# Where the taps of the convolution pause behind k, how LN2 spaces its last multiplications, when the sums of the next image are taken, and how the taps are shared out

## Chip, cores, metric

The kernel runs on one core of one Trainium2 chip. The metric is device time in microseconds of one execution; lower is better.

## What is computed

Eight images of 384 channels and 32 x 32 pixels pass through two layers. The first is an attention block over the 1024 pixels as tokens, the second a convolution block. Cut to what matters:

```python
# layer 0, tokens (1024 x 384), 8 heads of 48
xn = layernorm(x)                      # LN1
q, k, v = split(xn @ w_qkv.T + b_qkv)
out = softmax(q @ k.T * SCALE) @ v
x1 = x + out @ w_proj.T + b_proj
h = gelu(layernorm(x1) @ w_fc1.T + b_fc1)   # LN2, fc1: 384 -> 1536
x2 = x1 + h @ w_fc2.T + b_fc2               # fc2: 1536 -> 384
# layer 1
y = depthwise_conv_7x7(x2)             # 49 taps a channel
y = gelu(layernorm(y) @ w1 + b1)       # LN3, 384 -> 1536
y = grn(y) @ w2 + b2                   # global response norm, 1536 -> 384
out = x2 + y
```

All in fp32.

## The kernel before

**Tiling.** Channels lie on the 128 partitions in CT = 3 channel tiles, the 1024 tokens on the free axis in two halves of 512. A "product" below is TensorE work of U = 0.857 us in the plan: one full 128 x 128 matmul of 512 columns (the trace shows each as two records), or eight small matmuls of attention. Large linears use a scheme with 15 products in place of 18 blocks (`tiles_by_thirds`, `by_thirds`); q and k are made so, each in 15 products in the order `SINGLY` = 6, 10, 3, 5, 12, 2, 0, 11, 1, 4, 14, 7, 9, 8, 13. `behind(n)` is called with the number of the product, not with its place in that order: product 2 is the sixth, 0 the seventh, 7 the twelfth, 9 the thirteenth. The last two products of k are issued inside attention (`last_tile`). Results go out of the PSUM banks n, z, k, x by ScalarE copies (L470, L478) and VectorE adds (L473, L476); then a ScalarE bias (L648) finishes a whole tile of q or k.

**Order of the work.** [...]every engine runs its own list, and the lists are written by a planner, `Flow`. Each product adds its duration to `flow.now`; generators ("chains") hold the work of VectorE, ScalarE, POOL and DMA that goes on beside the products. A chain issues some instructions and yields how long it wants to wait; it is resumed behind the first product that ends past its due time. `flow.finish(chain)` issues the rest at once. So a number in a `yield` is not a wait on the chip, but a place in the lists.

**The stages of a middle image b (2 to 6).** The convolution of image b-1 runs beside the layer-1 linears of image b-2 and the first layer of image b: `grn_up` (w1), values of the image, `grn_down` (w2), q and k, attention (64 steps of scores, L804, Exp, L813, and product with v, L824), two `proj` (L746), LN2, fc1, fc2. VectorE and helpers share its 49 taps per channel tile:

- `convolution` issues VectorE taps (L1225, one tap of one channel tile of 1024 pixels each), paced by `us` and by `first`; it yields while the list `hold` is not empty.
- `help_convolution` takes the last `HELPED[ct]` taps of channel tile ct, tiles 2, 1, 0 in that order, in two halves each: ScalarE multiplies into one of four buffers (L1260) and POOL issues a DMA that accumulates it into `acc` (L1261). It pauses while the list `quiet` is not empty and three microseconds of plan beyond it; a tile is closed to `convolution` from the helper's first tap of it until 8 us after its last.
- `hold` is filled behind the twelfth product of k and emptied at the second scores of attention (`n == 1`); also in the two groups of the fast fc1 and over LN2 ("group", "ln2"). `quiet` is filled over `grn_down` and for two stretches of attention ("averages", from 23 and from 55 steps done), emptied behind each `proj`.

**LN2, the next image's LN1 and LN3.** `layernorm` makes a mean and a variance with matmuls against ones (L508; with folded halves L522), then three multiplications by scale and rstd (L582). In images 2 to 6 (`fast_fc1`) the second half of LN2 runs beside six plain fc1 tiles and the second `gelu_group` of 15 half-size products. Behind it stand, in this order: the adds of `norm_of_next` (LN1 of image b+1, L1967 and L1969), the end of the convolution (`end_convolution`: helper and taps finished at once), 11 us of plan, and LN3's adds (L541, L544), folds (POOL, L516), sums (L522), centring (L551), squares, variance. `norm_of_next(b, us)` takes its sums (L1961, four strips of 32 rows) `us` after its start, its variance later, and yields 45 us ahead of its final multiplications, which are needed by values of image b+1.

Of the kernel before, what the change touches and what calls it, by code (L numbers as in the profile page):

```python
# [64 lines left out]
CM = 2  # L65
NC = HT // CM
U = 0.857
HELPED = 6, 7, 7
BEGUN = 5
SCALE = HD ** -0.5  # L70
EPS0, EPS1, GRN_EPS = 1e-5, 1e-6, 1e-6
# [105 lines left out]
def block_kernel(  # L177
# [346 lines left out]
            totals.append((total, cols))  # L524
        return totals

    def layernorm(src, dst, h, eps, g, name, switch, spare=None, spaced=False, slow=1.0, fold=None, wait=3.4, gentle=False, late=0, lag=0, fold_squares=True):

        cols = h if isinstance(h, slice) else half(h)
        if isinstance(h, slice):
            h = h.start
        width = cols.stop - cols.start
        if spare:
            a, *squares = (t[:, :width] for t in spare())
            rstd = a
        else:
            a = one.tile([P, NH], F32, tag="ln_a", name=f"{name}_a{h}")[:, :width]  # L540
        nc.vector.tensor_tensor(a, src[:, 0, cols], src[:, 1, cols], ALU.add)  # L541
        if gentle:
            yield 1.2
        nc.vector.tensor_tensor(a, a, src[:, 2, cols], ALU.add)  # L544
        yield 2.6 * max(slow, 1.0)
        totals = yield from token_sums(a, f"{name}_sum{h}", fold, wait)
        yield 0.8
        for ct in range(CT):
            for total, part in totals:
                to, of = dst[:, ct, cols][:, part], src[:, ct, cols][:, part]  # L550
                nc.vector.scalar_tensor_tensor(to, total, -1.0 / C, of, ALU.mult, ALU.add)  # L551
            if gentle:
                yield 1.2
        yield 0.8 * slow + lag
        if not spare:
            squares = [three.tile([P, NH], F32, tag="ln_sq", name=f"{name}_sq{h}_{ct}")[:, :width] for ct in range(CT)]
        for ct in range(CT):
            nc.scalar.activation(squares[ct], dst[:, ct, cols], AF.Square)
            if spaced:
                yield 1.7  # L560
        yield 0.8 if spaced else 1.8 * slow
        nc.vector.tensor_tensor(squares[0], squares[0], squares[1], ALU.add)
        if gentle:
            yield 1.2
        nc.vector.tensor_tensor(squares[0], squares[0], squares[2], ALU.add)
        yield 1.8 * slow
        if not fold_squares:
            fold = None
            yield wait
        totals = yield from token_sums(squares[0], f"{name}_var{h}", fold, wait)  # L570
        yield 0.8

        if not spare:
            rstd = one.tile([P, NH], F32, tag="ln_rstd", name=f"{name}_rstd{h}")[:, :width]
        if switch:
            ln_table()
        for var, part in totals:
            nc.scalar.activation(rstd[:, part], var, AF.Ln, bias=eps, scale=1.0 / C)
        nc.scalar.activation(rstd, rstd, AF.Exp, scale=-0.5)
        yield (2.6 if switch else 1.2) * slow + late  # L580
        for ct in range(CT):
            nc.vector.scalar_tensor_tensor(dst[:, ct, cols], dst[:, ct, cols], col(g, ct), rstd, ALU.mult, ALU.mult)  # L582
            if gentle and ct < CT - 1:
                yield 1.2

    def averages():
        return [attn[:, i, :] for i in range(4)]
# [48 lines left out]
    def qk(b, xn, weights=None):  # L636

        big = large_tile(b)  # L640
        wqk_sb = wqk_in(big)
        parts = big[:, : 2 * NP * N].rearrange("p (i m n) -> p i m n", i=2, m=NP)
        moves = [(own, other) for i in range(2) for own, other in pieces(lambda m: parts[:, i, m, :])]

        def finish(i, m, src, cols=slice(0, N)):
            at = i * CT + m
            bias = bqk[:, at : at + 1]
            nc.scalar.activation(parts[:, i, m, cols], src, AF.Identity, bias=bias, scale=1.0 if i else SCALE)  # L648

        def move(i, m):  # L650
            for own, other in moves[2 * (i * CT + m) : 2 * (i * CT + m) + 2]:
                nc.sync.dma_start(out=own, in_=other)

        def args(i, m):
            return lambda k: wqk_sb[:, k, i * CT + m, :], lambda k: xn[:, k, :], CT

        def finishing(i, m):
            yield 1.7
            finish(i, m, parts[:, i, m, :])
            move(i, m)  # L660

        chains = {}

        def ready(m):

            for key in list(chains):
                if m in (key[1], NP - 1):
                    flow.finish(chains.pop(key))

        def plain(i, m):  # L670
            finish(i, m, linear(*args(i, m), f"qk_{b}_{i * CT + m}"))
            move(i, m)

        def fast(i):
            tiles = {}

            def bank(name):
                name = "x" if name in "jqm" else name
                if name not in tiles:
                    tiles[name] = o_tile(f"qk_{b}_{i}_{name}")  # L680
                return tiles[name]

            c = {f"c{r + 1}{n + 1}": parts[:, i, CT - 1 - r, half(n)] for r in range(CT) for n in range(2)}

            def behind(n):
                if i and n == 7:
                    hold.append("k")
                if n in (4, 9, 13):
                    m = (4, 9, 13).index(n)
                    chains[i, m] = flow.spawn(finishing(i, m))  # L690

            return tiles_by_thirds(weights, f"qk_{b}", i, thirds["qk"], c, bank, behind)

        def last_tile():

            if weights:
                flow.finish(rest_of_k)
                return
            for h in range(2):
                finish(1, CT - 1, linear_half(*args(1, CT - 1), h, f"qk_{b}_last_{h}"), half(h))  # L700
            move(1, CT - 1)

        if weights:
            for _ in fast(0):
                pass
            rest_of_k = fast(1)
            for n in rest_of_k:
                if n == 9:
                    break
            return parts[:, 0], parts[:, 1], last_tile, ready  # L710

        for m in range(CT):
            for i in range(2):
                if (m, i) != (CT - 1, 1):
                    plain(i, m)
        return parts[:, 0], parts[:, 1], last_tile, ready
# [76 lines left out]
    def attention(b, xt, qT, kT, last_tile, ready, first, next_image):  # L793
# [44 lines left out]
        for n in range(len(steps) + 2):  # L838
            if n == 1:
                hold.clear()  # L840
            if n == 2:
                last_tile()
            if n < len(steps):
                if steps[n][0] == 0 and steps[n][2] == 0:
                    ready(steps[n][1])
                ps[n] = scores(*steps[n])
            if n >= 2:
                product(*steps[n - 2], ps.pop(n - 2))
            if n - 2 in (len(steps) // 2 - 9, len(steps) - 9):
                quiet.append("averages")  # L850
            if n - 2 == len(steps) // 2 + 6:
                for chain in first:
                    flow.finish(chain)
                xn = one.tile([P, CT, N], F32, tag="xn", bufs=2, name=f"xn2_{b}")
                for m in (NP - 1, *range(CT)):
                    flow.finish(chains[0, m])
                proj(b, xt, 0)
                quiet.clear()
                next_image(b)
                slow = {1: 1.35, B - 1: 1.2}.get(b, 1.0)  # L860
                fold = "columns" if b else None
                ln = layernorm(xt, xn, 0, eps0, "g2", f"ln2_{b}", False, spaced=True, slow=slow, fold=fold, wait=4.5)
                if fast_fc1(b):
                    ln = sequence(ln, make_quarters(xn, hidden(b), 1.5))
                ln = flow.spawn(ln)
# [121 lines left out]
    def mlp(b, xt, xn, weights, tag, ln, rest, before_fc2=None, behind_ln=None):  # L987
# [9 lines left out]
        for m in range(HT // 2 if fast else HT):  # L997
# [5 lines left out]
            if m == (1 if fast else 3) and rest:  # L1003
                rest()
                slow = 0.8 if fast else 1.2 if b == 1 else 1.0
                if fast:
                    hold.append("ln2")
                ln = flow.spawn(layernorm(xt, xn, 1, eps0, "g2", f"ln2_{b}", True, slow=slow))
                behind_ln(ln)
        if fast:  # L1010
            gelu_group(hid, 1, b, weights, waiting)
# [817 lines left out]
    def main():  # L1829
# [60 lines left out]
        def conv_norm(b, ln):  # L1890
# [5 lines left out]
            else:  # L1896
# [1 line left out]
                how = dict(wait=5.0, late=3.5 if b > 1 else 0, fold_squares=b > 1) if b < B - 1 else dict(factor=2.4, slow=1.5, lag=4.0)  # L1898
                norm = abreast(acc, acc, eps1, "lnw", f"ln3_{b - 1}", True, **how)
                if b < B - 1:  # L1900
                    state["norm1"] = flow.spawn(after(ln, freely(norm_of_next(b, 22.0 if b > 1 else 28.0))))
                    state["norm3"] = flow.spawn(after(ln, freely(sequence(end_soon(b), norm))))
                else:
                    state["norm3"] = flow.spawn(after(ln, after(state["help"], after(state["conv"], norm))))
# [31 lines left out]
        def norm_of_next(b, us):  # L1936
# [62 lines left out]
            for h, a, _ in pairs:  # L1999
                for ps, view in sums[h]:  # L2000
                    nc.scalar.activation(view(a), ps, AF.Ln, bias=eps0, scale=1.0 / C)
                nc.scalar.activation(a, a, AF.Exp, scale=-0.5)
            yield 45.0
            for h, a, _ in pairs:
                for ct in range(CT):
                    part = xn[:, ct, half(h)]
# [257 lines left out]
```

## Time and profile before

| what | us |
|---|---|
| median of 3 runs | 3239.14 |
| lowest, highest | 3237.69, 3244.53 |
| profiled execution, its own time | 3245.64 |
| its span (first to last instruction) | 3243.9 |
| TensorE busy in it | 3213.5 (99%) |
| VectorE busy | 2540.3 (78%) |
| ScalarE busy | 1683.6 (52%) |
| POOL busy | 506.5 (16%) |
| all waits of TensorE for ScalarE at L648 / for VectorE at L473 | 8.6 / 8.0 |

The profile shows one execution. PE is TensorE, PEld its weight loads, DVE VectorE, ACT ScalarE, POOL GpSimd, SP the queue of most plain DMAs. A line of a timeline gives start, duration, engine, line of the kernel, operation, output <- input, shape, how many in a row, and in brackets the idle time ahead of it and what ended it. Matmuls overlap, so the time between two starts tells more than the durations. PEclk is the granted TensorE clock as a share of full speed.

### The profile page before, as it was taken

What the parts mean: (1) busy time and instruction counts of PE and PEld (TensorE: products, weight loads), DVE (VectorE), ACT (ScalarE), POOL (GpSimd) and SP (SyncE); (2) the same over time, 40 slices, a digit from 0 to 9 for tenths busy, and PEclk for the clock granted to TensorE, in tenths of its full rate; (3) what the DMA queues carried; (4) which work ended last, traced back from release to release, by engine and by line L of the source; (5) the groups of instructions that cost most, each with busy time, mean ns of one, the idle gap of its engine ahead of it and who ended that gap; (6) DMA issues with size and microseconds to landing.
All of it is one profiled execution on the core that took longest, in us unless ns stands there. A gap on an engine that the chain in (4) does not pass through costs nothing.

```text
span 3243.9 us, 39415 instructions
## 1 busy us (share of the span) xinstructions
PE 3213.5 (99%) x14204; PEld 1402.6 (43%) x14204; DVE 2540.3 (78%) x3578; ACT 1683.6 (52%) x2389; POOL 506.5 (16%) x607
## 2 busy tenths in 40 slices
PE   9999999999999999999999999999999999999999
PEld 5344434443444434444344443444435443344454
DVE  4548788897878978688777888778887788869964
ACT  3542763447644475453753637637375374742543
POOL 2102311012120121201212012120221202200000
PEclk9999999999999999999999999999999999999999
DMA  6525832557445564546636375363843638333244
GB/s 215 191 96 190 159 71 58 156 124 159 91 88 143 140 137 90 103 131 165 130 69 132 108 186 105 76 135 103 201 96 74 140 98 204 71 78 83 65 116 113
DMA packets 208741, 396.77 MB, mean 122 GB/s; under 512 B 42912, under 2 KB 49440, under 8 KB 208160
## 3 DMA queue, kind: packets, MB, share of 16 engines
q0 software_dynamic: 81984, 167.02, 27.2%
q1 hardware_dynamic: 126272, 226.49, 23.3%
q8 instruction: 114, 1.87, 0.2%
q10 hardware_dynamic: 288, 0.71, 0.1%
q14 instruction: 83, 0.68, 0.1%
HBM read 212.98 MB, written 40.11 MB: 78 GB/s over the span
## 4 chain that ended last, share of the span: by engine, by line
PE 86%; issue 5%; DMA 4%; DVE 3%; ACT 1%; POOL 1%; SPq 0%; POOLq 0%; DVEq 0%; ACTq 0%
PE fc L405 15%; PE s L804 13%; PE o L824 12%; PE fc_p L486 11%; PE o_p L486 6%; PE v L724 4%; PE proj L746 4%; PE h_n L457 3%; DMA acc<-tap 3%; PE h_z L457 3%; PE h_x L457 3%; PE h_last L1398 2%; PE o L1349 2%; PE h L392 2%; PE h_k L457 1%
## 5 line engine op out<-in xcount | busy, mean ns | idle before, releaser
L1225 DVE SCALAR_TENSOR_TENSOR acc<-pad,vec,acc 128x930 f32<-128x930 f32 (+8 forms) x808 | 905.5, 1157 | 5.7 <-DMA acc<-tap 2.5
L813 ACT ACTIVATE p<-s 128x1024 f32<-128x1024 f32 x512 | 523.9, 1025 | 250.3 <-PE s L804 242.3
L804 PE MATMUL s<-qk 48*64 48x512 f32 x4096 | 546.7, 592 | 10.0 <-ACT qk L648 8.6
L824 PE MATMUL o<-p,v 64*64 64x512 f32 x4096 | 541.8, 588 | 0.0
L405 PE MATMUL fc<-xn,fc 128*128 128x512 f32 x972 | 430.6, 599 | 0.0
L1261 POOL DMA_DIRECT2D acc<-tap x280 | 240.6, 873 | 1164.6 <-DVE gscale L1427 504.0
L486 PE MATMUL o_p<-y,w 128*128 128x512 f32 x664 | 289.0, 593 | 0.0
L804 PEld LDWEIGHTS s<-qk 48*64 48x64 f32 x4096 | 162.7, 133 | 289.1 <-issue 210.3
L405 PEld LDWEIGHTS fc<-xn,fc 128*128 128x128 f32 x972 | 185.5, 192 | 230.9 <-issue 224.6
L824 PEld LDWEIGHTS o<-p,v 64*64 64x64 f32 x4096 | 166.7, 132 | 274.3 <-issue 266.8
L486 PE MATMUL fc_p<-qk,fc 128*128 128x512 f32 x520 | 226.9, 593 | 0.0
L1260 ACT ACTIVATE tap<-pad,vec 128x512 f32<-128x512 f32 x280 | 206.3, 738 | 24.7 <-DMA acc<-tap 24.7
L486 PEld LDWEIGHTS o_p<-y,w 128*128 128x128 f32 x664 | 125.6, 190 | 157.7 <-issue 146.4
L1225 DVE SCALAR_TENSOR_TENSOR acc_last<-pad,vec,acc_last 128x377 f32<-128x377 f32 (+24 forms) x288 | 177.2, 688 | 0.6
L486 PEld LDWEIGHTS fc_p<-qk,fc 128*128 128x128 f32 x520 | 98.4, 190 | 123.6 <-issue 119.1
L498 ACT ACTIVATE qk<-fc,bfc_f 128x512 f32<-128x512 f32 x90 | 61.1, 684 | 141.9 <-PE fc L405 141.9
L498 ACT ACTIVATE hid<-fc,bfc_f 128x512 f32<-128x512 f32 x72 | 49.3, 687 | 159.1 <-PE fc L405 159.1
L765 DVE TENSOR_TENSOR attn<-o,attn 128x512 f32<-128x512 f32 x64 | 44.1, 689 | 110.9 <-ACT attn L763 109.2
L746 PE MATMUL proj<-attn,wproj_sb 128*128 128x512 f32 x288 | 127.3, 595 | 1.1 <-ACT b_f L1706 0.6
L974 ACT COPY pad<-x 128x512 f32<-128x512 f32 x42 | 26.4, 635 | 196.1 <-DVE x L1064 196.1
L724 PE MATMUL v<-wv_sb,xn 128*128 128x384 f32 x384 | 126.8, 487 | 0.0
L724 PEld LDWEIGHTS v<-wv_sb,xn 128*128 128x128 f32 x384 | 72.5, 190 | 50.1 <-issue 3.3
(445 smaller groups left out, 4610.3 us busy)
## 6 DMA issues: line engine op xcount, KB each, us to landing
acc<-tap POOLq DMA_DIRECT2D x280, 256.0 KB, 3.7
fc<-s_fc SPq DMA_DIRECT2D x91, 256.0 KB, 4.5
w<-s_w SPq DMA_DIRECT2D x91, 256.0 KB, 2.7
w<-s_w SPq DMA_DIRECT2D x72, 320.0 KB, 4.2
fc<-in_wfc SPq DMA_DIRECT2D x54, 384.0 KB, 4.2
y<-y POOLq DMA_DIRECT2D x38, 512.0 KB, 6.8
qk<-qk POOLq DMA_DIRECT2D x30, 512.0 KB, 7.4
qk<-s_qk SPq DMA_DIRECT2D x42, 320.0 KB, 5.1
```

Of the source, the lines that this page charges most:

```text
L405: nc.tensor.matmul(out=ps, lhsT=lhsT(k), rhs=rhs(k)[:, half(h)], start=(k == 0), stop=(k == nk - 1))
L457: nc.tensor.matmul(out=at, lhsT=weights.at(wname, g, slot // 5)[:, slot % 5, :], rhs=rhs[n], start=first, stop=True, skip_group_check=not ...
L486: nc.tensor.matmul(out=bank, lhsT=lhsT, rhs=rhs, start=k == 0, stop=k == len(pairs) - 1)
L498: nc.scalar.activation(dst, src, function, **kw)
L724: nc.tensor.matmul(out=ps[:, :C], lhsT=xn[:, k, t * P : (t + 1) * P], rhs=wv_sb[:, k, :], start=(k == 0), stop=(k == CT - 1),)
L746: nc.tensor.matmul(out=ps, lhsT=wproj_sb[:, m, ct * P : (ct + 1) * P], rhs=attn[:, m, :], start=(m == 0), stop=(m == CT - 1),)
L804: nc.tensor.matmul(out=s[64 * i : 64 * i + 64, j, :], lhsT=kT[64 * j : 64 * j + HD, m, k0 : k0 + 64], rhs=qT[64 * j : 64 * j + HD, m, half ...
L813: nc.scalar.activation(p, s, AF.Exp)
L824: nc.tensor.matmul(out=outs[i][64 * j : 64 * j + 64, :], lhsT=v[keys, t, at : at + 64], rhs=p[keys, j, :], start=(t == 0), stop=(t == KT - 1),
L1225: nc.vector.scalar_tensor_tensor(dst, window, tap, dst, ALU.mult, ALU.add)
L1260: nc.scalar.mul(t.rearrange("p (h w) -> p h w", w=W), window, tap)
L1261: nc.gpsimd.dma_start(out=acc[:, ct, half(h)], in_=t, accum_op=ALU.add)
```

## The change

Five edits. In the second half of `fast` (k), the helper is paused (`quiet`) behind product 2, the sixth, and the VectorE taps (`hold`) behind product 0, the seventh, instead of the VectorE taps alone behind product 7, the twelfth; both lists are emptied at the second scores. `HELPED` goes from 6, 7, 7 to 5, 7, 7, so that VectorE makes 44, 42 and 42 taps instead of 43, 42 and 42. LN2's three last multiplications of the second half are issued 1.3 us of plan apart in images 2 to 6 instead of in a row. The next image's sums are due 25 us instead of 22 us behind the start of its norm in images 2 to 6. Its final multiplications are due 42 us instead of 45 us behind the rstd, in images 1 to 6.

```diff
-HELPED = 6, 7, 7
+HELPED = 5, 7, 7
...
-    def layernorm(src, dst, h, eps, g, name, switch, spare=None, spaced=False, slow=1.0, fold=None, wait=3.4, gentle=False, late=0, lag=0, fold_squares=True):
+    def layernorm(src, dst, h, eps, g, name, switch, spare=None, spaced=False, slow=1.0, fold=None, wait=3.4, gentle=False, late=0, lag=0, fold_squares=True, apart=0):
...
             nc.vector.scalar_tensor_tensor(dst[:, ct, cols], dst[:, ct, cols], col(g, ct), rstd, ALU.mult, ALU.mult)
-            if gentle and ct < CT - 1:
-                yield 1.2
+            if (gentle or apart) and ct < CT - 1:
+                yield apart or 1.2
...
             def behind(n):
-                if i and n == 7:
+                if i and n == 2:
+                    quiet.append("k")
+                if i and n == 0:
                     hold.append("k")
...
             if n == 1:
                 hold.clear()
+                quiet.clear()
...
-                ln = flow.spawn(layernorm(xt, xn, 1, eps0, "g2", f"ln2_{b}", True, slow=slow))
+                ln = flow.spawn(layernorm(xt, xn, 1, eps0, "g2", f"ln2_{b}", True, slow=slow, apart=1.3 if fast else 0))
...
-                    state["norm1"] = flow.spawn(after(ln, freely(norm_of_next(b, 22.0 if b > 1 else 28.0))))
+                    state["norm1"] = flow.spawn(after(ln, freely(norm_of_next(b, 25.0 if b > 1 else 28.0))))
...
-            yield 45.0
+            yield 42.0
```

## The prediction

> **What bounds the kernel now.** I read the page first, for the engine that has no time left.
>
> ```profile
> PE 3213.5 (99%) x14204; PEld 1402.6 (43%) x14204; DVE 2540.3 (78%) x3578; ACT 1683.6 (52%) x2389; POOL 506.5 (16%) x607
> ```
>
> TensorE is busy for 3213.5 of 3243.9 us. The change removes no product, so it can win only TensorE's 30.4 us of idle time and whatever is hidden in "busy". The waits of TensorE, longest in total first, say where the idle time is:
>
> ```profile
> PE s L804 <- ACT qk L648: 8.6, 7, 2.4
> PE fc_n L457 <- DVE qk L473: 8.0, 5, 1.6
> PE ln_sum L1961 <- PE ln_sum L1961: 1.7, 5, 0.4
> ...
> PE s L804 <- ACT p L813: 1.4, 4, 0.5
> ```
>
> (total us, times, longest.) The first stands at the step from k to attention in the seven images 1 to 7, the next two in the images 2 to 6 that use the fast fc1. I then read the timeline at each place. Image 3, step to attention:
>
> ```profile
> 1143.62 0.74 ACT L1260 ACTIVATE tap<-pad,vec 128x512 f32<-128x512 f32 x1 [1.67 <-DMA acc<-tap]
> 1144.73 0.59 ACT L478 COPY qk<-qk_x 128x512 f32<-128x512 f32 x1
> 1145.35 0.69 DVE L473 TENSOR_TENSOR qk<-qk_n,qk 128x512 f32<-128x512 f32 x1 [2.49 <-ACT qk L478]
> 1147.85 0.74 ACT L1260 ACTIVATE tap<-pad,vec 128x512 f32<-128x512 f32 x1 [2.53 <-DMA acc<-tap]
> 1148.49 1.13 ACT L648 ACTIVATE qk<-qk,bqk 128x1024 f32<-128x1024 f32 x1
> 1149.68 1.95 PE L804 MATMUL s<-qk 48*64 48x512 f32 x16 [1.96 <-ACT qk L648]
> ```
>
> A helper's tap on ScalarE (L1260) waits for the landing of an older tap; the k copy and the bias (L648) that the first score needs stand behind it. The LN2 place, image 4:
>
> ```profile
> 1703.95 2.07 DVE L582 SCALAR_TENSOR_TENSOR xn<-xn,vec,ln_rstd 128x512 f32<-128x512 f32 x3
> 1705.93 0.41 DVE L473 TENSOR_TENSOR qk<-fc_n,qk 128x256 f32<-128x256 f32 x1
> 1706.40 0.70 PE L457 MATMUL fc_n<-xn,fc1t 128*128 128x256 f32 x2 [1.61 <-DVE qk L473]
> ```
>
> Three LN2 multiplications in a row delay the eviction (L473) that frees bank n. Last, the table of stretches (length, busy of PE, PEld, DVE, ACT, POOL, then PEclk) shows time that is called busy:
>
> ```profile
> 941.00:944.60 3.60, 3.60 (x6) 1.51 (x7) 3.60 (x7) 1.26 (x2) 0.00 (x0) 0.53 0.00 0
> 1738.00:1741.50 3.50, 3.50 (x10) 1.50 (x9) 3.50 (x8) 1.43 (x3) 0.00 (x0) 1.00 0.10 14
> 2736.60:2743.50 6.90, 6.66 (x20) 1.98 (x20) 2.31 (x3) 5.81 (x7) 2.54 (x3) 0.51 0.84 146
> ```
>
> After LN3's sums (L522) and the next image's sums (L1961), which stand back to back, the clock is about half for some 3.4 us in image 2 (first row), and likewise from 1340.5 (0.51) and 2528.4 (0.50), but not in image 4 (second row). The third row is the longest k wait, image 7: half the clock for 6.9 us.
>
> [...]
>
> **The change, part by part.** I followed the emission plan by hand (products of 0.857, taps and chains at their due times). For the old kernel it gives what the trace has: ten taps in the last burst, and the last helper tap just ahead of score 57 of the second pause.
>
> *Pauses behind k.* The ScalarE taps stop after the sixth product of k's second half, the VectorE taps after the seventh; until now ScalarE's never stopped and VectorE's stopped after the twelfth. Three helper taps (halves) and two VectorE taps move behind the first scores. The copy and the add of c31 then follow their products: product 10 ends 1144.7, add 0.69 with 0.17 ahead, L648 1.15: done by 1146.8, while TensorE is through its thirteenth product at 1147.2. The first score waits for nothing. From the end of the thirteenth product to the first score I read 0.1, 0.7, 2.1, 1.4, 1.5, 1.0 and 2.6 us (images 1 to 7), and 0.3 lost just before in image 3: **-9.7**. In image 7 the four products from the first score on took 7.0 us (2736.84 to 2743.85) against 3.8 in image 4, the halved clock: **-3.2**. The table load runs 1.5 us earlier, so the Exp waits (1.4, 2.2 with drains) shrink: **-1.3**. ScalarE's queue ahead of its next Exp is then as in image 1, where no Exp is late.
>
> *HELPED.* Per image two L1260 (0.738) and two POOL issues (0.873) go, one L1225 (1.157) comes; seven images: -10.3 on ScalarE, -12.2 on POOL, +8.1 on VectorE. None of the three ends a wait here by its sum. But the pause costs the helper about 10 us and the missing tap gives back 5 (two halves, 2.5 apart): by the plan 36 of 38 halves are issued before the pause at score 57, and two fall behind the second proj, during LN2, where ScalarE idles 2.3 us ahead of its squares. Price 0; without that idle time at most 0.74 for each.
>
> *The burst.* What VectorE has not done when LN2 ends is issued at once: ten taps now, twelve after (one counts as due just before). That is 2 x 1.157 = 2.3 us later for LN3's adds, their folds on POOL (L516), and TensorE's L522:
>
> ```profile
> 1713.66 11.57 DVE L1225 SCALAR_TENSOR_TENSOR acc<-pad,vec,acc 128x841 f32<-128x841 f32 x10
> 1728.81 1.33 POOL L516 DMA_DIRECT2D ln_a<-ln_a  x1
> 1729.36 1.62 POOL L516 DMA_DIRECT2D attn<-attn  x1
> 1734.62 1.07 PE L522 MATMUL ln_sum<-ln_a,ones 64*64 64x512 f32 x4
> ```
>
> The folds take 5.5 and 6.2 us to land because a 512 KB fc_e transfer (issued 1728.07, landed 5.3 later) is ahead of them; alone they take 3.4 to 3.6. The adds end 1726.7 and 1728.0; 2.3 later the folds go out near 1729.1 and 1730.4 and still end behind fc_e. Cover about 2 us: **+0.2** an image, +1; bounds 0 and 2.3 an image.
>
> *LN2 apart.* The adds of bank n then follow one multiplication (0.69): ready 1704.97 instead of 1706.35; the product waits 0.4 instead of 1.77 (1706.40 less its own 1704.63). The third multiplication ends near 1708.4, the first product that reads it comes after 1710: 5 x 1.3 = **-6.5**.
>
> *Next image's sums.* Due at 25 instead of 22, L1961 falls two full products behind L522. Its fourth product waits 0.35 for LN3's first centring (one bank serves both); that is then past: **-1.7**. [...]three half-clock windows at 3.4 x 0.5: **-5.1** in this execution. Everything of that norm moves with it: nine centrings (3.86), squares, two folds and four second folds of squares on POOL, ahead of fc2's own accumulates with about 3 us to spare. LN3's squares now precede them. Behind them wait bank s0 for fc2's first product and the gelu of fc1's tile 10: **+0.3** an image (+1.5), bounds 0 and 1.5. The multiplications stay at 67 for images 2 to 6 and come 3 us earlier in image 1, with no reader near: 0.
>
> Sum: -9.7 - 3.2 - 1.3 - 6.5 - 1.7 - 5.1 + 1 + 1.5 + 0.5 for the wider ScalarE/DMA reshuffle = **-24.5**. The profiled execution took 3245.64 (span 3243.9 and 1.7 around it), so 3221. It stands 6.5 above the median, 3239.14; its four clock drops, 8.3 us, can differ in each run, as three runs 6.8 apart suggest. Taken from the median with the fixed part (-19.2 + 3) and 3.4 for two drops: 3219.5. I take **3219.5**.
>
> **The rivals.** *Part comes back:* the two added taps show in full at L522 (2.3) and s0 is late (1.5) in five images: 19 instead of the 2.5 in my sum, 3219.5 + 16.5 = 3236, and 3228 where half of it shows. For it: VectorE runs without a gap from 1702 to 1728. Against: the fc_e transfer sets the landing now. *The pause doesn't empty ScalarE:* taps already queued still wait for landings, as the 0.95 ahead of the tap at 1140.72 shows; half of the k gain stays, 3219.5 + 7 = 3226.5. Against: that tap ends before the sixth product does. *Slower:* the two helper halves stay blocked until the burst. Its channel-tile-0 tap then waits for multiply, issue and landing, 0.74 + 0.87 + 3.7 = 5.3 us, and with the two added taps L522 comes 7.6 - 2 = 5.6 us late, in five images +28: 3239 - 19 + 28 = 3248. It decides where the second half has not landed when VectorE reaches that tap, the fifth of the burst, near 1719. By the plan it is issued 13 us of products before the burst, which speaks against. A *same* result needs some 3.3 us an image given back.
>
> **How the numbers follow.** Forecast 0.68, given back 0.12, half emptied 0.08, slower 0.07, near nothing 0.05. Runs of this kernel can tell a change of about 0.2%, 6.5 us. The first three lie beyond it mostly: faster 0.86, same 0.07, slower 0.07. The range 3211 to 3233 takes in all clock drops gone and no new cost (3239 - 19.2 - 8.3 = 3211.5), and rather more than half of the given-back case.
>
> **What the profile after would show.** Right: s <- qk L648 gone from TensorE's waits; fc_n <- qk L473 at 2 us or less in five; no half clock after the sums; TensorE busy near 3202 and a span near 3219; twelve or eleven taps in the burst; two taps on ScalarE in LN2. Wrong: TensorE waiting at L522 for a landing, fc2's first product waiting for xn's centring, or L648 still late.

## The result, and the profile after

The changed kernel takes **3221.03 us** (median of four runs, 3218.43 to 3224.02) beside 3241.84 for the kernel before in the same series: ratio as recorded 0.9931, 95% interval 0.9913 to 0.9949 (the two medians alone would give 0.9936). Forecast were 3219.5, with 3211 to 3233 as the range. The profiled execution took 3218.43, forecast 3221 for it, from 3245.64. The same kernel measured once more in a later series (e5 below) gave 0.9931 (0.9917 to 0.9946).

Line numbers move in the kernel after: scores L804 are L806, Exp L813 L815, taps L1225, L1260 and L1261 are L1228, L1263 and L1264, the next image's sums L1961 are L1964. L457, L473, L516, L522, L541, L582 and L648 stay.

First the page, busy time and share of each engine:

```profile
span 3216.7 us, 39370 instructions
PE 3201.6 (100%) x14204; PEld 1404.2 (44%) x14204; DVE 2547.9 (79%) x3585; ACT 1676.8 (52%) x2375; POOL 494.0 (15%) x593
```

The span is 27.2 us shorter. TensorE does the same 14204 matmuls in 11.9 us less busy time, and its idle time is halved, from 30.4 to 15.1. Most of the busy time is the clock: before, four stretches of 3.4, 3.4, 3.4 and 6.8 us ran at half clock and so lost 8.5 us; after, none did (the last 2 to 4 us of either kernel apart). TensorE's waits after, in total us, times and longest:

```profile
PE fc_n L457 <- DVE qk L473: 1.6, 6, 0.3
PE ln_var L522 <- DMA ln_sq<-ln_sq: 1.4, 2, 0.8
...
PE ln_sum L522 <- DMA attn<-attn: 0.6, 3, 0.2
PE ln_sum L522 <- DMA ln_a<-ln_a: 0.4, 1, 0.4
...
PE s L806 <- ACT qk L648: 0.2, 1, 0.2
```

The first score's wait fell from 8.6 to 0.2 (a wait in image 0, which was there before too), that of fc_n from 8.0 to 1.6; the wait inside the next image's sums and that for the Exp are gone. New are two waits at L522 for the folds, 1.0 in all. The timeline at the step to attention in image 3:

```profile
1140.48 0.69 DVE L473 TENSOR_TENSOR qk<-qk_n,qk 128x512 f32<-128x512 f32 x1 [1.95 <-PE qk_n L457]
1141.21 1.15 ACT L648 ACTIVATE qk<-qk,bqk 128x1024 f32<-128x1024 f32 x1 [1.07 <-DVE qk L473]
1142.38 1.28 ACT L494 ACT_TABLE_LOAD   x1
1142.88 1.95 PE L806 MATMUL s<-qk 48*64 48x512 f32 x16
1144.04 1.02 ACT L815 ACTIVATE p<-s 128x1024 f32<-128x1024 f32 x1 [0.38 <-PE s L806]
```

The bias L648 now waits for VectorE's add and for nothing else; it ends at 1142.36, the table load of 1.28 us follows it on ScalarE, and the first score starts at 1142.88 without a bracket, that is, without a wait. LN2 in image 4:

```profile
1689.78 0.74 DVE L582 SCALAR_TENSOR_TENSOR xn<-xn,vec,ln_rstd 128x512 f32<-128x512 f32 x1
1690.44 0.41 DVE L473 TENSOR_TENSOR qk<-fc_n,qk 128x256 f32<-128x256 f32 x1
1690.91 0.70 PE L457 MATMUL fc_n<-xn,fc1t 128*128 128x256 f32 x2 [0.28 <-DVE qk L473]
...
1691.98 0.74 DVE L582 SCALAR_TENSOR_TENSOR xn<-xn,vec,ln_rstd 128x512 f32<-128x512 f32 x1
```

One multiplication stands ahead of the eviction in place of three, and the product waits 0.28 instead of 1.61. Then the end of LN2, with the burst (the taps that VectorE has not done when LN2 ends, issued at once), LN3's adds, the fold and its reader:

```profile
1696.32 1.18 DVE L1228 SCALAR_TENSOR_TENSOR acc<-pad,vec,acc 128x930 f32<-128x930 f32 x1
...
1699.83 12.15 DVE L1228 SCALAR_TENSOR_TENSOR acc<-pad,vec,acc 128x870 f32<-128x870 f32 x11
1712.01 0.69 DVE L541 TENSOR_TENSOR ln_a<-acc 128x512 f32<-128x512 f32 x1
1712.58 1.19 POOL L973 DMA_DIRECT2D fc_e<-qk  x1 [3.94 <-ACT fc_e L972]
1714.62 0.85 POOL L516 DMA_DIRECT2D ln_a<-ln_a  x1 [0.86 <-DVE attn L541]
1719.57 1.08 PE L522 MATMUL ln_sum<-ln_a,ones 64*64 64x512 f32 x4 [0.38 <-DMA ln_a<-ln_a]
```

Eleven taps stand in the burst and a twelfth just ahead of it (first line), where the kernel before has ten and none: the twelve of the prediction, with the one that it counts as due just before. LN3's adds start 0.56 us ahead of the fc_e transfer's issue, before 2.81 ahead: 2.25 later, forecast 2.3. Last the table of stretches, with length, busy time of PE, PEld, DVE, ACT and POOL, then PEclk; two of image 2, from the next image's sums on, at the times at which the kernel before stood at half clock:

```profile
938.80:942.20 3.40, 3.27 (x15) 1.37 (x14) 3.24 (x6) 2.86 (x6) 0.00 (x0) 1.00 0.28 77
942.20:945.60 3.40, 3.40 (x9) 1.52 (x8) 3.19 (x8) 2.77 (x6) 1.43 (x2) 1.00 0.21 33
```

No half clock is left at the sums or behind k.

### The profile page after: what moved, and what is told of

It is laid out like the page before. It is cut to its first block, busy times and chain, and to the rows that moved or that the text cites. A ratio compares the mean times of both kernels' runs of the same rounds, so it can differ in the third digit from the quotient of the medians.

```text
span 3216.7 us, 39370 instructions
## 1 busy us (share of the span) xinstructions
PE 3201.6 (100%) x14204; PEld 1404.2 (44%) x14204; DVE 2547.9 (79%) x3585; ACT 1676.8 (52%) x2375; POOL 494.0 (15%) x593
## 4 chain that ended last, share of the span: by engine, by line
PE 92%; DMA 3%; issue 2%; DVE 1%; POOL 1%; ACT 1%; SPq 0%; POOLq 0%; DVEq 0%; ACTq 0%
PE fc L405 14%; PE s L806 12%; PE o L826 12%; PE fc_p L486 11%; PE o_p L486 11%; PE proj L748 4%; PE v L726 3%; PE h_n L457 3%; PE h_z L457 3%; PE h_x L457 2%; PE h_last L1401 2%; PE o L1352 2%; PE h L392 2%; PE qk_n L457 2%; PE qk_z L457 2%
## 5 line engine op out<-in xcount | busy, mean ns | idle before, releaser
L1228 DVE SCALAR_TENSOR_TENSOR acc<-pad,vec,acc 128x870 f32<-128x870 f32 (+8 forms) x815 | 911.1, 1157 | 2.7
L815 ACT ACTIVATE p<-s 128x1024 f32<-128x1024 f32 x512 | 524.3, 1025 | 256.7 <-PE s L806 248.1
L806 PE MATMUL s<-qk 48*64 48x512 f32 x4096 | 539.8, 590 | 0.2 <-ACT qk L648 0.2
L1264 POOL DMA_DIRECT2D acc<-tap x266 | 226.6, 857 | 1361.9 <-ACT tap L1263 678.8
L806 PEld LDWEIGHTS s<-qk 48*64 48x64 f32 x4096 | 163.9, 132 | 272.9 <-issue 206.0
L1263 ACT ACTIVATE tap<-pad,vec 128x512 f32<-128x512 f32 x266 | 195.1, 736 | 2.8 <-DMA acc<-tap 2.8
L1228 DVE SCALAR_TENSOR_TENSOR acc_last<-pad,vec,acc_last 128x377 f32<-128x377 f32 (+24 forms) x288 | 177.2, 690 | 0.6
```

The lines of the kernel that those rows point to most:

```text
L806: nc.tensor.matmul(out=s[64 * i : 64 * i + 64, j, :], lhsT=kT[64 * j : 64 * j + HD, m, k0 : k0 + 64], rhs=qT[64 * j : 64 * j + HD, m, half ...
L815: nc.scalar.activation(p, s, AF.Exp)
L1228: nc.vector.scalar_tensor_tensor(dst, window, tap, dst, ALU.mult, ALU.add)
L1263: nc.scalar.mul(t.rearrange("p (h w) -> p h w", w=W), window, tap)
L1264: nc.gpsimd.dma_start(out=acc[:, ct, half(h)], in_=t, accum_op=ALU.add)
```

## The experiments

Three series of four kernels; the kernel before ran beside each of them (medians 3246.0, 3245.1 and 3244.4), so ratios to it compare across series. One thing blurs medians of this kernel: near 140 us, in image 0, `proj` waits up to 3.2 us for VectorE's L793 (L791 in the kernel before), and a half-clock stretch of up to 6.8 us comes and goes behind it, whatever the kernel. So the table also gives, from each profile, the time from the first score of image 1 to the end of the span ("rest"), which leaves image 0 out. Medians of different series differ by a few us for the same kernel; the ratios allow for that.

| kernel | median us | ratio, 95% interval | rest |
|---|---|---|---|
| before (profile) | 3241.84 | | 2887.1 |
| after (profile) | 3221.03 | 0.9931, 0.9913 to 0.9949 | 2860.4 |
| e1: k's pauses undone | 3232.94 | 0.9960, 0.9947 to 0.9973 | 2875.1 |
| e2: LN2 not apart | 3225.05 | 0.9938, 0.9924 to 0.9953 | 2866.3 |
| e3: sums at 22 | 3222.97 | 0.9930, 0.9916 to 0.9945 | 2859.7 |
| e4: 6, 7, 7 helped | 3220.67 | 0.9922, 0.9907 to 0.9936 | 2858.6 |
| e5: after again | 3222.52 | 0.9931, 0.9917 to 0.9946 | 2860.9 |
| e6: ScalarE's pause only | 3222.55 | 0.9933, 0.9919 to 0.9947 | 2860.3 |
| e7: VectorE's pause only | 3236.05 | 0.9974, 0.9967 to 0.9982 | 2877.6 |
| e8: halves in the burst | 3227.89 | 0.9953, 0.9939 to 0.9966 | 2867.7 |
| e9: 3, 7, 7 helped | 3224.33 | 0.9938, 0.9925 to 0.9950 | 2863.7 |
| e10: before with sums at 25 | 3241.88 | 0.9992, 0.9984 to 1.0000 | 2886.4 |
| e11: before again | 3246.67 | 1.0006, 0.9998 to 1.0015 | 2883.7 |
| e12: ScalarE's pause, 6 helped | 3220.72 | 0.9929, 0.9916 to 0.9942 | 2861.8 |

### One part undone at a time

**e1**, the pauses behind k as before, all else changed:

```diff
-                if i and n == 2:
-                    quiet.append("k")
-                if i and n == 0:
+                if i and n == 7:
                     hold.append("k")
...
                 hold.clear()
-                quiet.clear()
```

> The changed kernel with the pauses behind k put back as they were (VectorE's taps alone pause, behind the twelfth product). Sum theory: the waits at the first scores come back, 9.7 us, with 1 us of late Exps, and in some executions 3.2 us of half clock in one image: 11 to 14 us slower than the changed kernel's 3221, so about 3233, and 9 faster than the kernel before. TensorE's wait s <- qk L648 is 7 to 10 us over seven images again. Rival (clock alone: all of the gain is half-clock windows gone, and removed waits only move): within 3 us of 3221. Plan: eleven taps in the last burst instead of twelve, no tap in LN2.

Measured 3232.94, the rest 14.7 longer than after; the first score waits 9.8 us for L648 (longest 3.6) and 1.3 for the Exp, and a half-clock stretch of 6.8 us stands at the first scores of image 3 (before: of image 7). The pauses behind k are about half of the gain: 14.7 of 26.7 us in the rest, 9.4 of 22 us by the ratios.

**e2**, LN2's multiplications in a row again:

```diff
-..., True, slow=slow, apart=1.3 if fast else 0))
+..., True, slow=slow, apart=0))
```

> The changed kernel with LN2's three multiplications in a row again. Sum theory: 5 x 1.3 = 6.5 us slower than the changed kernel, about 3227.5; the profile has fc_n <- qk L473 at 1.6 each, five times. Rival (a wait taken away there shows up later in fc1 or fc2, since VectorE is the engine behind): under 2 us slower.

Measured 3225.05, the rest 5.9 longer, and fc_n waits 8.2 us for L473 instead of 1.6. The two profiles say 6 us; the medians say 2.5 to 4, with intervals that hold both.

**e3**, the next image's sums at 22 again, the multiplications at 45 behind them:

```diff
-... norm_of_next(b, 25.0 if b > 1 else 28.0) ...
+... norm_of_next(b, 22.0 if b > 1 else 28.0) ...
...
-            yield 42.0
+            yield 45.0
```

> The changed kernel with the next image's sums at 22 and the final multiplications at 45 again. Sum theory: the 0.35 wait five times, 1.7 us, and half-clock windows after the sums in about three of five images, 5 us: 5 to 8 us slower, about 3228, with a wider spread between runs; the table of stretches shows PEclk near 0.5 at one to four of the five places. Rival (the windows come from chance, not from the place): 1 to 2 us slower and no half clock.

Measured 3222.97; the rest is 0.7 shorter. L1964 waits 0.5 us in all, and no half clock followed the sums in any image. In this place the edit bought nothing that shows in this run; why, is taken up with e10 and e11.

**e4**, six helped taps for channel tile 0 again:

```diff
-HELPED = 5, 7, 7
+HELPED = 6, 7, 7
```

> The changed kernel with six helped taps of channel tile 0. By the plan four helper halves instead of two fall into LN2, the last two ahead of ScalarE's rstd, and the last burst has eleven taps. Sum theory: 0 to 4 us slower (two taps of 0.74 in LN2's chain in five images, less one VectorE tap). Rival (this edit carries a good part of the gain by taking load from ScalarE and DMA): 5 us or more slower.

Measured 3220.67, the rest 1.8 shorter, and an interval that holds the 0.9931 of after: no gain of this edit shows either.

### Which of the two pauses it is

**e6** leaves VectorE's pause at the twelfth product, **e7** leaves ScalarE's out; **e5** is the changed kernel beside them.

```diff
# e6                                 # e7
-                if i and n == 0:    -                if i and n == 2:
+                if i and n == 7:    -                    quiet.append("k")
```

> The changed kernel itself, so that the next three stand beside it on one chip. 3221 (3218 to 3225); TensorE idle about 15 us, no wait of the first score for L648 above 0.3 us. If its gain came only from half-clock windows that happened to fall well, it would spread by several us and come near 3228 at times.

> Of the two pauses behind k only ScalarE's is moved (after the sixth product); VectorE's taps stop after the twelfth as before. My theory: the copy and the bias were late because they stood behind ScalarE taps that waited for landings, so this half holds nearly the whole gain: 3221 to 3224, eleven taps in the burst, s <- qk L648 at most 2 us. Rival, that both engines hold up the chain alike: the add of k (L473) falls behind a VectorE tap of 1.16 us in most images, L648 is late by about 1 us in seven, 3228.

> Of the two pauses only VectorE's is moved (after the seventh product); ScalarE's taps never stop behind k, as before. My theory: nothing gained over the kernel without both moves (3233), waits s <- qk L648 at 7 to 10 us, and twelve taps in the burst with cover for them: 3231 to 3235. Rival, both engines alike: half of the wait gone, 3227.

e6 is as fast as e5 (3222.55 and 3222.52), e7 13.5 slower. The timeline of e7 at image 3 shows the cause in the tap at 1144.95:

```profile
1140.41 0.58 ACT L478 COPY qk<-qk_x 128x512 f32<-128x512 f32 x1 [0.26 <-PE qk_x L457]
...
1144.95 0.74 ACT L1261 ACTIVATE tap<-pad,vec 128x512 f32<-128x512 f32 x1 [3.96 <-DMA acc<-tap]
1145.60 1.13 ACT L648 ACTIVATE qk<-qk,bqk 128x1024 f32<-128x1024 f32 x1
1146.79 3.33 PE L804 MATMUL s<-qk 48*64 48x512 f32 x16 [2.98 <-ACT qk L648]
```

ScalarE stands idle for 3.96 us, because a tap at the head of its queue waits for a buffer whose accumulate has not landed; the bias behind it has had its data since 1142.03, when VectorE's add ended. The scores that then start take 3.33 for what is 1.95 at full clock. In e6 a VectorE tap is back beside k's last adds, and costs nothing:

```profile
1142.22 1.18 DVE L1228 SCALAR_TENSOR_TENSOR acc<-pad,vec,acc 128x930 f32<-128x930 f32 x1
1142.34 1.15 ACT L648 ACTIVATE qk<-qk,bqk 128x1024 f32<-128x1024 f32 x1 [1.07 <-DVE qk L473]
1143.31 0.68 DVE L473 TENSOR_TENSOR qk<-qk_z,qk 128x512 f32<-128x512 f32 x1
1143.91 0.68 DVE L476 TENSOR_TENSOR qk<-qk,qk_k 128x512 f32<-128x512 f32 x1
1144.01 1.95 PE L806 MATMUL s<-qk 48*64 48x512 f32 x16
```

The tap follows the add that L648 needs and delays only later adds, and no first score waits (0.2 us for L648 in all, in image 0). The rival that both engines count alike (3228 for e6, 3227 for e7) falls.

### The burst, its cover, and the slower rival

**e8** makes the slower rival true: in images 2 to 6 the pause of ScalarE's taps ends only when the burst is issued, so the two late halves go out in it.

```diff
-            quiet.clear()
+            if not fast_fc1(b):
+                quiet.clear()
...
+                if fast_fc1(b):
+                    quiet.clear()
                 flow.finish(state["help"])
                 flow.finish(state["conv"])
```

> The changed kernel with the pause of ScalarE's taps not ended after score 57's stretch in the five images of the fast fc1, but only when the burst is issued: the helper's last halves go out in the burst, as in my slower rival. By that rival's own price the fold at L522 comes 5.6 us late in five images: 3221 + 28 = 3249, with TensorE waiting at L522 for a landing about 5 us in each. If VectorE does not stand at the tap of channel tile 0 (the half landed, or its order in the burst leaves time), the delay is that of the landing alone beyond the cover of 2 us: at most 1.7 in each, 3229. If the burst has more cover than I reckoned: 3221.

**e9** lengthens the burst with nothing else late: HELPED = 3, 7, 7.

> The changed kernel with 3, 7, 7 helped taps in place of 5, 7, 7: the burst at the end of LN2 grows from eleven to fourteen taps, VectorE reaches LN3's adds 3 x 1.157 = 3.5 us later. By the cover in my prediction (2 us, of which the eleventh tap has taken 1.2) L522 comes 2.7 us late in five images: 3221 + 13 = 3234. By the cover that the run with the blocked halves showed (3.6 us late, 1.3 of it at L522, so 2.3 left) it is 1.2 in each, 3227. If the length of the burst costs nothing at all: 3221.

e8 first, the burst in image 4 on VectorE, POOL and TensorE:

```profile
1705.42 4.23 DVE L1229 SCALAR_TENSOR_TENSOR acc<-pad,vec,acc 128x870 f32<-128x870 f32 x4
1712.89 8.03 DVE L1229 SCALAR_TENSOR_TENSOR acc<-pad,vec,acc 128x928 f32<-128x928 f32 x7 [3.24 <-DMA acc<-tap]
...
1723.55 0.85 POOL L516 DMA_DIRECT2D ln_a<-ln_a  x1 [4.18 <-issue]
...
1726.41 1.07 PE L522 MATMUL ln_sum<-ln_a,ones 64*64 64x512 f32 x4 [1.63 <-DMA ln_a<-ln_a]
```

VectorE stops at the fifth tap of the burst, the place that the rival named. But the stop is 3.24 us and not 5.3, although the landing takes 5.4 us where the price had 3.7: ScalarE multiplies from 1702.66 on, and the first four taps run while the halves travel. TensorE then waits 1.63. In all five images, from its waits:

```profile
PE ln_sum L522 <- DMA ln_a<-ln_a: 7.5, 5, 2.3
```

That is 7.5 us, where 28 were priced; the rest is 7.3 longer than after. In e9 the burst has thirteen taps, not fourteen: LN3's adds start 1.61 us behind fc_e's issue, 2.2 later than after and not 3.5. TensorE waits 2.0 us in five images; the rest is 3.3 longer, the median 3224.33. The prices of 13 and of 6 us were both too high. Why, is in the landing times of the fold (queue totals around the burst in image 4: KB each, us from issue to landing), of after, e9 and e8:

```profile
ln_a<-ln_a POOLq DMA_DIRECT2D x1, 128.0 KB, 4.8
```

```profile
ln_a<-ln_a POOLq DMA_DIRECT2D x1, 128.0 KB, 3.2
```

```profile
ln_a<-ln_a POOLq DMA_DIRECT2D x1, 128.0 KB, 2.7
```

The later the fold went out behind the 512 KB fc_e transfer in these three, the sooner it landed. fc_e is issued at 1712.58 after and at 1716.11 in e9, and lands 5.1 and 5.2 later; the fold is issued 2.0 and 3.6 behind fc_e, and lands 1.8 and 1.6 behind fc_e's landing, so 6.8 behind its issue in both. Only in e8, issued 5.4 behind it, does its own 2.7 count. TensorE is ready for L522 6.6 us behind fc_e's issue in all three. So the wait has three parts. A fold issued 0.74 behind fc_e (before) or 1.4 (four of the five images after) cost nothing; issued 2.0 behind it (image 4 after) it cost 0.38 us and 3.6 behind it (image 4 of e9) 0.3, and the longest of the five waits is 0.6 in e9; issued 5.4 behind it (image 4 of e8) it cost 1.63, and the longest wait of e8 is 2.3. From these numbers I estimate that every further microsecond counts from about 6.6 - 2.7 = 3.9 on. From the 0.74 of before, the cover is then about 3.2 us and not 2, at a price of about half a microsecond at most.

### What the sums' place is worth

**e10** is the kernel before with e3's edit the other way round (25 and 42), **e11** the kernel before again.

> The kernel before with one part of the change alone: the next image's sums at 25 in place of 22, the multiplications at 42 after them. By my sum: the wait of 1.7 us inside the sums gone and the half-clock windows behind them gone, 5.1 in a run that has three: 3.4 to 6.8 below the kernel before, 3239. Rival, that the windows fall on the place by chance (about one in three of five places) and that only the wait goes: 1 to 4 below, 3242. The waits at k and at LN2 stay at about 8.6 and 8.0 us.

> The kernel before once more, for its half-clock windows: in the first profile they followed the sums in three images of five. If the place of the sums makes them, they come again in the same three images (2, 3 and 6). [...]

e10 is 2.6 us faster than before by the ratio (0 to 5.2), in the range of the lower expectation, though the interval reaches into the other's; its wait inside the sums is gone, and those for L648 (9.2) and at fc_n (8.0) stand as before. e11 shows how the clock differs from run to run. In the first profile of before half-clock stretches followed the sums of images 2, 3 and 6; in this one it is image 6 alone. TensorE there, then the stretch behind the sums in image 6, and the end of the sums with what follows in image 3:

```profile
2528.59 1.08 PE L522 MATMUL ln_sum<-ln_a,ones 64*64 64x512 f32 x4
2529.71 1.08 PE L522 MATMUL ln_sum<-attn,ones 64*64 64x512 f32 x4
2530.72 0.71 PE L1961 MATMUL ln_sum<-ln,ones 32*128 32x256 f32 x6
2531.70 0.80 PE L1961 MATMUL ln_sum<-ln,ones 32*128 32x256 f32 x2 [0.27 <-PE ln_sum L1961]
2532.43 7.79 PE L405 MATMUL fc<-xn,fc 128*128 128x512 f32 x14
```

```profile
2532.00:2535.40 3.40, 3.40 (x6) 1.42 (x5) 3.40 (x7) 1.26 (x2) 0.00 (x0) 0.52 0.00 0
1343.00:1346.40 3.40, 3.02 (x15) 1.16 (x12) 3.40 (x7) 0.00 (x0) 0.00 (x0) 1.00 0.00 0
1346.40:1349.80 3.40, 3.40 (x10) 1.49 (x9) 3.40 (x9) 2.70 (x5) 0.00 (x0) 1.00 0.27 80
```

No full product runs from 2528.59 to 2532.43, 3.84 us; call this the dip. The next 3.4 us are at half clock. The dip is in the same place in all five images; whether a half-clock stretch follows differs from run to run. Of 15 such places in the three profiles with the sums at 22 (before, e3, e11) four had one; of 55 in the eleven with the sums at 25, one. That one is e8's image 3, where TensorE first waits:

```profile
1331.21 1.08 PE L522 MATMUL ln_sum<-ln_a,ones 64*64 64x512 f32 x4 [1.67 <-DMA ln_a<-ln_a]
1332.24 1.12 PE L522 MATMUL ln_sum<-attn,ones 64*64 64x512 f32 x4
1333.29 3.59 PE L405 MATMUL fc<-xn,fc 128*128 128x512 f32 x4
```

1.67 of idle time and 2.1 of small sums make a dip of 3.75 us (1329.54 to 1333.29), and PEclk is 0.52 from 1333.0 to 1336.4.

The profile of before has a record of each change of the granted clock. Its half-clock stretches start at 941.236, 1340.595, 2528.433 and 2736.646 us and last 3.413, 3.413, 3.413 and 6.827 us; the distances between their starts are 117, 348 and 61 times 3.4133. So in this profile they all lie on one grid with steps of 3.4133 us.

The five dips of this profile, in images 2 to 6, are 3.91, 3.71, 3.70, 3.69 and 3.85 us long. In images 2 and 6 a whole step of the grid lies within the dip (937.82 to 941.24 and 2525.02 to 2528.43), in image 3 all but the last 0.34 us of one, and the half clock starts where that step ends. In images 4 and 5 the step that comes nearest begins 1.5 and 0.7 us ahead of the dip, and the clock stays full. At 25 the dips are shorter: 2.2 to 2.6 us in the profile of after, where no half clock follows any. That is what the edit does for the clock, besides the wait of 1.7 us. That place and chance both have a part, the one by the length of the dip, the other by where the grid lies in a run, is my estimate from these five dips; for the other profiles it is not shown. In e3 the sums are back at 22, the dip of image 2 is 3.70 us long (936.57 to 940.27), and no half clock follows it or the other four.

### The smaller change

**e12** keeps of the change only what paid or was not tried apart: VectorE's pause at the twelfth product, 6, 7, 7 helped taps.

> The changed kernel less the two parts that bought nothing: VectorE's pause behind k back at the twelfth product, and 6, 7, 7 helped taps. From the two runs that undid them one at a time: 3220 to 3222, no difference from the changed kernel that can be measured. If the two parts needed each other (a VectorE tap ahead of k's add, and more helper halves late in LN2) it is slower, 3226.

Measured 3220.72, ratio 0.9929. No difference from the changed kernel can be measured: it is as fast with two edits fewer.

## Why the prediction was right, point by point

**Pauses behind k, -14.2: right in size and in mechanism.** By e1 it is 14.7 in the rest, 11.9 in the median and 9.4 by the ratio; by e7 against e5, which differ in ScalarE's pause alone, 16.7 in the rest and 13.5 in the median. Of its terms, the waits for L648 and Exp were 8.4 and 1.4 in the trace (9.7 and 1.3 in the sum). The prediction puts the seven waits of 8.6 us on images 1 to 7; they are those of images 2 to 7 and one of 0.2 in image 0, which stays. The term for the halved clock, 3.2, was read from one place in one execution; the five profiles without ScalarE's pause lose 3.4 to 6.8 there, in image 3, 7 or both, and the nine with it nothing. It was the right size for a single run, and the image that it falls on differs between the five. The sum did not divide the two pauses; e6 shows that VectorE's is worth nothing.

**HELPED, 0: right, as far as can be told.** e4 lies 0.4 below after in the median, 2.9 by the ratio and 1.8 in the rest; its interval holds the ratio of after, so neither a gain nor a loss is shown. Two ScalarE taps did fall into LN2, in its idle time.

**Burst, +0.2 an image: right, with its cover mis-sized.** L522 waits 1.0 us in all, 0.2 an image, and VectorE is 2.25 us later, as the sum had it. The reason was the right one too: the fc_e transfer ahead sets the landing (the fold lands 6.8 us behind fc_e's issue in after and in e9). But the cover is about 3.2 us, by my estimate, and not 2, since the first fold alone lands in 2.7 us (e8) and not in 3.4 to 3.6. The small waits stand within the cover (0.4 us in image 4, the rest at the second fold), and not at its end, where the sum had them; that both came to 0.2 an image is luck.

**LN2 apart, -6.5: right by the traces.** fc_n's wait fell by 6.4; e2 gives 5.9 in the rest, and 2.5 to 4 in medians whose intervals hold 6.5.

**Next image's sums, -6.8: the term that was mis-sized.** The wait of 1.7 is gone (e10's and the changed kernel's waits). The -5.1 for three half-clock stretches is what these two executions differ by, but as the worth of the edit it is too much: the sum took the stretches as made by the place alone, and e3 has the sums there and none, e11 one. The full products between the sums did shorten the dips, from 3.7 to 3.9 us before to 2.2 to 2.6 after, and no half clock followed them in after. By the count, 4 of 15, five images have 1.3 of them on average, at half of 3.4 us each 2.3 us, a rough estimate from three profiles; e10 has 2.6 for wait and clock together (0 to 5.2), where the sum had 6.8 from the execution and 5.1 from the median.

**Bank s0 and gelu behind the moved work, +1.5: not there.** TensorE's waits show none for fc2's first product.

**The sum.** The profiled execution became 27.2 us shorter, forecast were 24.5. The two costs that did not come, 2 us at s0 and in the reshuffle, are most of the difference in size. By kind it fits less well: busy time fell by 11.9 where the clock terms had 8.3, idle time by 15.3 where the waits had 19.2 less 3 of new ones; the 3.6 more of busy time I can't assign to a line. The median fell by 18.1 from the 3239.14 that the forecast started from, 19.6 forecast; that start was a low draw of three, and beside runs of the same series it is 20.8 to 22.6.

**The rivals.** *Part comes back:* no, L522 waits 1.0 in all. *The pause doesn't empty ScalarE:* no, the last tap ahead of the bias of image 3 waited 0.58 us for a landing, but started at 1136.02, five us ahead of the bias. *Slower:* its stop at the fifth tap is real (e8), but the halves were issued in time, and its price was nearly four times too high (28 for 7.5 us): it let multiply, issue and landing start only when VectorE was already waiting, and kept the cover at 2.

## What to carry over

ScalarE worked its list in order in these timelines: in e7 it stood idle for 3.96 us at a tap, with the bias behind it whose data had been there since 1142.03. A list that mixes critical copies with filler that may wait on a transfer should have no filler before the critical stretch; ask which of the engines holds filler that can *block*, because filler that only takes time (VectorE's taps here, 3222.55 in e6 beside 3222.52 in e5) did no harm. The fold that queued behind the larger fc_e transfer could be issued later at little cost (at most 0.6 us in e9, up to 2.3 in e8, where its own landing time counted), so measure cover from the transfer ahead. A half-clock stretch in one trace is one draw (4 of 15 like places here had one): compare the dip ahead of it with the dip that the change leaves (3.7 to 3.9 us and 2.2 to 2.6 here), and count over several profiles before the stretch is priced as removable.

## What was not expected of the hardware

TensorE's clock was halved behind dips of 3.7 to 3.9 us without any full product, although small matmuls filled most of them (in e11's image 6 all but some 0.3 us), and not behind every such dip: 4 of 15 like places. Half clock came at late first scores too: in each of the five profiles without ScalarE's pause, in image 3, 7 or both, with waits for L648 of at most 2.4 to 3.6 us. In the profile of before it started in image 7, 0.19 us before the score that had waited 2.43 us, and lasted 6.83 us; in image 3, where the score waited 1.96, the clock stayed full. In the nine profiles with ScalarE's pause no score waited more than 0.2 us for L648, and no half clock stood behind k. Why small matmuls left the clock halved behind some of these dips and not behind others is not shown.
